# A message-passing layer: where TensorE makes a node block's two products, ahead of the node product of layer one or behind layer two

## The chip, the cores and the metric

The kernel runs on one core of one Trainium2 chip. The metric is the time of one execution on the device, in microseconds (us); lower is better. An engine runs its own instructions in the order in which they were written: TensorE (PE, with weight loads as PEld), VectorE (DVE), ScalarE (ACT), GpSimd (POOL), and SyncE (SP), which only issues DMAs here. They wait for each other through semaphores.

## The reference, cut to what matters

```python
gates = (ssp(edge_state @ We1 + be1) @ We2 + be2) * soft_cutoff      # 200000 edges, 64 wide
nodes = node_state[edges].reshape(num_edges, -1)                     # x[src] beside x[dst]
h = ssp(nodes @ Wn1 + bn1) @ Wn2 + bn2
messages = h * gates
message_sum = jnp.zeros_like(node_state).at[edges[:, 1]].add(messages)
new_state = node_state + (ssp(message_sum @ Ws1 + bs1) @ Ws2 + bs2)  # 12500 nodes, 64 wide
x = _layernorm(x + new_state, axis=-1)
```

`ssp(v)` is `softplus(v) - log 2`. The edges come sorted by `dst`, and low nodes have many more edges than high ones.

## The kernel before, in words

The 200000 edges are cut into 391 groups of 512. A loop makes one step for each group; in step `i` the engines work on several groups at once: the gathers of group `i + 3`, layer one of `i + 1`, layer two of `i`, and the scatter of `i - 2`. Nothing is reordered: `manual_schedule` makes each engine's queue follow the source.

What TensorE does in step `i`, in its order before the change:

- L299 and L342: the biases of layer one for `i + 1` (`layer1_bias`) and of layer two for `i` (`layer2_bias`).
- L371 (`scatter`): the messages of group `i - 2` times one-hot columns. DVE adds the result into the table `sums` (L391, `window`, two adds for a group).
- L286 (`transposes`): the gathered rows of group `i + 1` are turned into the PSUM tile `tx`. ACT copies them to SBUF (L294, `xcopy`).
- L304 (`layer1_edge`): the edge product of layer one.
- L337 (`busy_before_node`): a product that nobody reads, made in 221 of the steps, those for which `four(i + 5)` holds (all four rows of a later group are gathered, none is made from columns), from step 91 on. In the steps before that, L641 (`chunk`) stands here: a piece of a table that is built meanwhile.
- L311 (`layer1_node`): the node product of layer one, which reads what L294 copied; in some steps with L314, for rows that DVE and ACT made from columns of `x` (L262, 16 small copies a step on either engine, chosen by L274).
- L349 and L354 (`layer2`): the products of layer two for group `i`, which read the softplus that DVE wrote a step earlier (L333).

POOL does nothing but issue gathers (L204), three or four a step. ACT does L294, its 16 column copies, then the exponential (L325) and the logarithm (L328) of what L311 made. DVE does the two adds into `sums`, the cut and the message (L363, L367, which read layer two), softplus (L333), the one-hot (L280), its column copies.

The nodes are finished in 25 blocks (a first one of 212 nodes, the rest 512). A block begins when the last edge that points into it has been added into `sums`. Its work is a list of parts; `BLOCK_STEPS` says how many steps later each part is done. Two of the parts have a TensorE product: `hidden` (L410, two products of 128x256 that read `sums`; one for the first block), two steps after the block's last edge, and `layer2` of the block (L438, a bias, and L441, two products of 128x128 that read `l_s`, the ssp that DVE wrote in L433), four steps after `hidden`. In a step that has such a part, the list `early` holds it; `part.tensor(tx_tile())` issues the product into a tile of the `tx` ring, and `part.others()` what DVE does with it (L425 and L426, or L445). 24 of the blocks are done within the loop, so 48 of its steps have one product each; the last block comes behind the loop and uses `gh` tiles.

```python
    def busy_before_node(g):
        nc.tensor.matmul(zs[g][:, 1, :HE], we1..., consts[:, :HE], start=True, stop=True, ...)
```

Of the kernel before, what the change touches and what calls it, by code (L numbers as in the profile page):

```python
# [34 lines left out]
AHEAD = 3  # L35
# [5 lines left out]
BEHIND = 5  # L41
# [14 lines left out]
def node_blocks(N):  # L56

    first = N % NB
    assert N > NB and first % 2 == 0 and first <= HE
    sizes = ([first] if first else []) + [NB] * (N // NB)  # L60
    return [(sum(sizes[:i]), n) for i, n in enumerate(sizes)]


def block_steps(N, NG):

    steps = []
    for at, n in node_blocks(N):
        share = sqrt(min(1.0, (at + n) / N))
        spread = sqrt(share * (1.0 - share) / (NG * GE))
        steps.append(ceil(NG * (share + SPREADS * spread)))  # L70
    return steps
# [33 lines left out]
def gnn_resnorm_kernel(ctx: ExitStack, tc: tile.TileContext, a: dict, out: bass.AP, E: int):  # L105
# [30 lines left out]
    def tx_tile():  # L136
        return psum.tile([P, NB], F32, name="tx")
# [54 lines left out]
    def padding(g, k):  # L192
        return g * GE + k % 2 * HE + k // 2 * P >= E
# [15 lines left out]
    def four(g):  # L209
        return g < NG and not any(padding(g, k) or (g, k) in by_columns for k in range(K))  # L210
# [270 lines left out]
    with tc.manual_schedule():  # L481
# [180 lines left out]
        with tc.tile_pool(name="finish", bufs=1) as finish:  # L662
            blocks = list(zip(node_blocks(N), block_steps(N, NG)))
            last = NG - 1
            parts, begun, complete, rest = {}, None, 0, []

            def at(f, g, *more):
                if 0 <= g < NG:
                    f(g, *more)

            def behind_by(i):
                close = last - CLOSE
                return [g for g in ([i - 2] if i <= close else []) + ([i - 1] if i >= close else []) if g >= 0]

            for g in range(LOADS - 1):
                load(g)
            for g in range(2):
                onehot(g)
            lowest(1, NR)
            everywhere(1, NR)  # L680
            clear(0, CHUNKS)
            highest()
            for i in range(-1, last - 1):
                now = parts.pop(i, [])
                early = [part for part in now if part.tensor]
                at(load, i + LOADS)
                if i >= 0:
                    at(gather, i + AHEAD, range(K), [("transposes", i)] if i < BEHIND else ())
                layer1_bias(i + 1)
                at(layer2_bias, i)  # L690
                for n, g in enumerate(behind_by(i)):
                    scatter(g, zs[i + 1][:, 1, HE + 2 * n * W : HE + 2 * (n + 1) * W])
                transposes(i + 1, ("load", i + 1), ("gather", i + 1), ("onehot", i + 1))
                xcopy(i + 1)
                columns(i, 1, finish)
                layer1_edge(i + 1)
                c = chunk_of(i, NCH)
                if c is None and four(i + AHEAD + BEHIND - 3):
                    busy_before_node(i + 1)
                if c is not None:  # L700
                    beside_sums = zs[i + 1][:, 1, HE + 2 * W : HE + 2 * W + P]
                    chunk(c, beside_sums)
                layer1_node(i + 1)
                exps(i + 1)
                logs(i + 1)
                if c is not None:
                    keep_chunk(c, beside_sums)
                read_columns(i + 1, 1)
                for g in behind_by(i):
                    window(g)  # L710
                if c is not None:
                    clear(c, c + 1)
                at(layer2, i)
                for part in early:
                    part.tensor(tx_tile())
                at(hcut, i)
                at(message, i)
                softplus(i + 1)
                for part in early:
                    part.others()  # L720
                at(onehot, i + 3)
                read_columns(i, 0)
                columns(i, 0, finish)
                choose(finish)
                for part in now:
                    if not part.tensor:
                        part.others()
                for action in beside.get(i, []):
                    action()
                complete = i  # L730
                if blocks and complete >= blocks[0][1] - PREPARE and not begun:
                    begun = node_block(*blocks[0][0], finish)
                    begun.pop(0).others()
                if blocks and complete >= blocks[0][1]:
                    steps = next(steps for steps in BLOCK_STEPS if i + steps[-1] < last - 1)
                    for n, part in zip(steps, begun):
                        parts.setdefault(i + n, []).append(part)
                    rest = begun[len(steps) :]
                    blocks.pop(0)
                    begun = None  # L740
            assert len(blocks) == 1 and begun and not parts


            begun.pop(2).others()
            transposes(last, ("load", last), ("gather", last), ("onehot", last))
            xcopy(last)
            layer1_bias(last)
            layer2_bias(last - 1)
            scatter(last - 2, zs[last][:, 1, HE : HE + 2 * W])
            layer1_edge(last)  # L750
            layer1_node(last)
            for some in (edge, node):
                exps(last, some)
                logs(last, some)
            square, variance, root, scale, store = (part.others for part in rest)
            square()
            window(last - 2)
            for g in range(last - 1, last + 1):
                if g not in window_at:
                    window_bases(g)  # L760
            layer2(last - 1)
            layer2_bias(last)
            softplus(last, edge)
            layer2_edge(last)
            softplus(last, node)
            layer2_node(last)
            hcut(last - 1)
            message(last - 1)
            scatter(last - 1, tx_tile()[:, : 2 * W])
            variance()  # L770
            root()
            hcut(last)
            message(last)
            scatter(last, tx_tile()[:, : 2 * W])
            window(last - 1)
            window(last)
            hidden, clamp = begun.pop(0)
            hidden(gh_tile())
            scale()
            clamp()  # L780
            store()
            for part in begun:
                node_part(part)
# [5 lines left out]
    with tc.If(far > 0), tc.tile_pool(name="outside", bufs=1) as o:  # L789
# [7 lines left out]
        with tc.For_i(0, NG, 1) as g:  # L797
# [51 lines left out]
            for b in range(NBL):  # L849
# [5 lines left out]
                part = sums[:D, b * NB : (b + 1) * NB]  # L855
# [90 lines left out]
```

## Time and profile before

| | us |
|---|---|
| median of three runs | 2354.70 |
| lowest and highest of the three | 2352.55, 2364.48 |
| the profiled execution, whole | 2351.35 |
| its span, first to last instruction | 2349.3 |

| engine | busy us | share |
|---|---|---|
| PE | 1986.8 | 85% |
| PEld | 1549.9 | 66% |
| DVE | 1536.7 | 65% |
| ACT | 1511.8 | 64% |
| POOL | 1391.5 | 59% |

The mean granted TensorE clock was 0.964 of full speed. In the profile a line such as "L410 PE MATMUL tx<-sums,consts" names the source line, the engine, the operation, and what it writes and reads. A group's row gives its count, busy time, mean duration of one record in ns, and the engine's idle time ahead of it with what ended that. A product in f32 leaves two records, so the 47 products of `hidden` are 94 records. In a timeline, the first two columns are the start and the length in us; brackets hold the idle time before.

### The profile page before, as it was taken

The numbers are of one execution on the slowest core, as the hardware profiler recorded it, in microseconds if no ns is written. First come the engines' busy times: TensorE is split into PE (matmuls) and PEld (weight loads), VectorE is DVE, ScalarE is ACT, GpSimd is POOL, SyncE is SP. The second block draws the span as 40 slices with busy tenths as digits, with TensorE's granted clock in tenths as the row PEclk, the third lists the DMA queues.
The fourth block names the chain that finished last, engine by engine and source line by source line (L and its number), as shares of the span: only waits on it lengthen the run. The fifth ranks groups of instructions, "written<-read, shape, count | busy, mean of one in ns | idle before, by whom it ended". The sixth has DMA issues, their size and how long they took to land.

```text
span 2349.3 us, 49245 instructions
## 1 busy us (share of the span) xinstructions
PE 1986.8 (85%) x12011; PEld 1549.9 (66%) x12011; DVE 1536.7 (65%) x9110; ACT 1511.8 (64%) x7412; POOL 1391.5 (59%) x1473
## 2 busy tenths in 40 slices
PE   6788888888888888888888888888888888888877
PEld 4676666666666666666666666666666666666665
DVE  4467666666666666666666667666666676667655
ACT  3466667666666666666667667666666666666653
POOL 6556666566666566666656566665666665556550
PEclk8799999999999999999999999999999999999988
DMA  6332232322222222222222222222222222222220
GB/s 190 95 83 71 64 70 57 79 62 74 60 59 57 54 62 54 59 56 61 55 58 63 52 61 63 59 59 58 59 59 59 59 61 60 55 56 59 60 51 13
DMA packets 162385, 149.51 MB, mean 64 GB/s; under 512 B 40564, under 2 KB 112021, under 8 KB 161962
## 3 DMA queue, kind: packets, MB, share of 16 engines
q1 hardware_dynamic: 114650, 96.55, 15.1%
q0 software_dynamic: 47008, 48.23, 10.9%
q8 instruction: 101, 1.65, 0.3%
q14 instruction: 192, 1.57, 0.2%
q10 hardware_dynamic: 434, 1.50, 0.2%
HBM read 136.50 MB, written 9.62 MB: 62 GB/s over the span
## 4 chain that ended last, share of the span: by engine, by line
PE 76%; issue 12%; DVE 6%; ACT 2%; DVEq 2%; another core or an unknown queue 1%; DMA 1%; POOL 0%; ACTq 0%; POOLq 0%
PE z L311 17%; PE gh L354 13%; PE z L371 10%; PE tx L286 9%; PE gh L349 8%; PE z L304 6%; PE z L337 4%; PE gh L342 3%; PE z L299 3%; DVE column L262 2%; DVEq L245 2%; ACT xT L294 1%; PE tx L410 1%; PE z L314 1%
## 5 line engine op out<-in xcount | busy, mean ns | idle before, releaser
L204 POOL DMA_INDIRECT xg<-in_x,src_i x1469 | 1391.3, 947 | 905.6 <-PE tx L286 378.3
L294 ACT COPY xT<-tx 106x512 f32<-106x512 f32 x391 | 228.6, 585 | 736.1 <-PE tx L286 704.6
L311 PE MATMUL z<-xT,wns 106*128 106x256 f32 x1564 | 464.1, 416 | 270.5 <-issue 238.0
L262 ACT COPY column<-xh 128x4 uint8 x6016 | 608.8, 193 | 0.0
L311 PEld LDWEIGHTS z<-xT,wns 106*128 106x128 f32 x1564 | 273.8, 197 | 420.4 <-issue 336.4
L262 DVE COPY column<-xh 128x4 uint8 x6016 | 486.4, 199 | 11.9 <-issue 6.9
L363 DVE TENSOR_TENSOR h<-gh,cut 128x256 f32<-128x256 f32 x391 | 166.0, 425 | 380.3 <-PE tx L286 260.8
L354 PE MATMUL gh<-consts,s 128*128 128x64 f32 x3128 | 400.2, 272 | 0.0
L354 PEld LDWEIGHTS gh<-consts,s 128*128 128x128 f32 x3128 | 389.6, 196 | 0.1
L328 ACT ACTIVATE u<-u,one 128x768 f32<-128x768 f32 x392 | 365.8, 933 | 13.5 <-ACT u L325 0.8
L333 DVE SCALAR_TENSOR_TENSOR s<-u,z 128x768 f32<-128x768 f32 x392 | 369.3, 942 | 0.4 <-issue 0.3
L391 DVE TENSOR_TENSOR sums<-sums,z 64x42 f32 x778 | 149.4, 192 | 325.5 <-issue 243.1
L325 ACT ACTIVATE u<-z 128x768 f32<-128x768 f32 x392 | 314.7, 803 | 47.2 <-PE z L311 25.5
L371 PEld LDWEIGHTS z<-xg,msg 128*128 128x128 f32 x1556 | 208.9, 195 | 140.9 <-issue 123.4
L371 PE MATMUL z<-xg,msg 128*128 128x84 f32 x1556 | 269.9, 297 | 13.6 <-DVE msg L367 13.5
L349 PEld LDWEIGHTS gh<-consts,s 128*128 128x128 f32 x1564 | 218.8, 196 | 92.7 <-DVE s L333 68.3
L349 PE MATMUL gh<-consts,s 128*128 128x128 f32 x1564 | 269.8, 296 | 11.8 <-issue 7.2
L286 PE MATMUL tx<-consts,xg 128*106 128x128 f32 x1564 | 243.9, 280 | 0.0
L304 PE MATMUL z<-eT,consts 128*128 128x256 f32 x782 | 243.7, 395 | 0.0
L286 PEld LDWEIGHTS tx<-consts,xg 128*106 128x106 f32 x1564 | 187.1, 145 | 1.2 <-issue 1.2
L367 DVE TENSOR_TENSOR msg<-gh,h 128x256 f32<-128x256 f32 x391 | 165.9, 424 | 13.4
L342 PE MATMUL gh<-row,ones 3*128 3x512 bf16 x391 | 149.3, 382 | 0.0
(107 smaller groups left out, 1193.4 us busy)
## 6 DMA issues: line engine op xcount, KB each, us to landing
eT<-in_eT SPq DMA_DIRECT2D x195, 256.0 KB
xg<-in_x,src_i POOLq DMA_INDIRECT x1469
wns<-table SPq DMA_DIRECT2D x782, 21.0 KB
table<-tb SPq DMA_DIRECT2D x14, 448.0 KB
side<-in_sides SPq DMA_DIRECT2D x94, 64.0 KB
y<-in_x SPq DMA_DIRECT2D x24, 128.0 KB
out<-y SPq DMA_DIRECT2D x24, 128.0 KB
xh<-in_xh SPq DMA_DIRECT2D x2, 781.5 KB
```

The costliest lines, as they stand in the source:

```text
L204: behind(note(("gather", g), nc.gpsimd.indirect_dma_start(out=xg[:, k, :D], out_offset=None, in_=x, in_offset=bass.IndirectOffsetOnAxis(ap ...
L262: copy(column_tiles[slot].bitcast(U8)[:, 4 * r : 4 * r + 4], xh[:, bass.ds(column_at[queue][j] - xh_at, 4)])
L286: ins = nc.tensor.transpose(tx[:, k, :], xgs[g][:, k, :DW], ident)
L294: note(("xcopy", g), nc.scalar.copy(xT, xTs[g]))
L304: nc.tensor.matmul(zs[g][:, 0, :HE], we1.rearrange("a h d -> a (h d)"), eTs[g], start=False, stop=True, skip_group_check=True)
L311: nc.tensor.matmul(zn, wns[:, g % REST, h, :], xTs[g][:, h], start=True, stop=not chosen, skip_group_check=True)
L325: nc.scalar.activation(us[g][:, part], z_of(g)[:, part], AF.Exp)
L328: nc.scalar.activation(us[g][:, part], us[g][:, part], AF.Ln, bias=one)
L333: nc.vector.scalar_tensor_tensor(ss[g].rearrange("p i t e -> p (i t e)")[:, part], us[g][:, part], BIG, z_of(g)[:, part], OP.min, OP.max)
L349: nc.tensor.matmul(v[:, 0, t], ss[g][:, 0, t, :], we2, start=False, stop=False, skip_group_check=True)
L354: nc.tensor.matmul(ghs[g][:, 1, 2 * t + h, :], ss[g][:, 1 + h, t, :], wn2, start=False, stop=h == 1 and t == 1, skip_group_check=True)
L371: ins = nc.tensor.matmul(sc, msgs[g][:, 2 * t : 2 * t + 2, :].rearrange("p h f -> p (h f)"), xgs[g][:, 2 * t : 2 * t + 2, D:DW], start=t = ...
```

## The change

In the 48 steps with a block's product, the product is issued between the edge product L304 and the node product L311 of layer one, where it stood behind layer two (L354). The unread product L337 is not made in such a step, where it was made before.

```diff
                 layer1_edge(i + 1)
                 c = chunk_of(i, NCH)
-                if c is None and four(i + AHEAD + BEHIND - 3):
+                for part in early:
+                    part.tensor(tx_tile())
+                if c is None and not early and four(i + AHEAD + BEHIND - 3):
                     busy_before_node(i + 1)
                 if c is not None:
                     beside_sums = zs[i + 1][:, 1, HE + 2 * W : HE + 2 * W + P]
...
                 at(layer2, i)
-                for part in early:
-                    part.tensor(tx_tile())
                 at(hcut, i)
                 at(message, i)
                 softplus(i + 1)
```

The unread product is made 221 times before and 190 times after: 31 of the 48 steps had it. The other 17 gain a product in that place.

TensorE's queue around a step with `hidden` (L410), before; the names are those of the tiles: `z` layer one, `gh` layer two, `tx` the transposes and the blocks, `xT` what ACT copied:

```order
L371 MATMUL z<-xg,msg 128x84 x2
L286 MATMUL tx<-consts,xg 106x128 x4
L304 MATMUL z<-eT,consts 128x256
L337 MATMUL z<-consts 128x256
L311 MATMUL z<-xT,wns 128x256 x2
L349 MATMUL gh<-consts,s 128x128 x2
L354 MATMUL gh<-consts,s 128x64 x4
L410 MATMUL tx<-sums,consts 128x256 x2
L299 LDWEIGHTS be_82
```

The same step with the change:

```order
L371 MATMUL z<-xg,msg 128x84 x2
L286 MATMUL tx<-consts,xg 106x128 x4
L304 MATMUL z<-eT,consts 128x256
L410 MATMUL tx<-sums,consts 128x256 x2
L311 MATMUL z<-xT,wns 128x256 x2
L349 MATMUL gh<-consts,s 128x128 x2
L354 MATMUL gh<-consts,s 128x64 x4
L299 LDWEIGHTS be_82
```

L410 takes the place of L337, and L299 of the next step follows layer two at once. Since the adds into `sums` of step `i` (L391) are written behind this place, L410 now reads `sums` as the adds of step `i - 1` left it; by then the block's last edges are in.

DVE's queue in such a step, with the semaphores that each row waits for, before:

```order
L391 TENSOR_TENSOR sums<-sums,z 64x42 [waits Activation_49]
L391 ISA
L391 TENSOR_TENSOR sums<-sums,z 64x42
L363 TENSOR_TENSOR h<-gh,cut 128x256 [waits PE_49]
L367 TENSOR_TENSOR msg<-gh,h 128x256 [waits DVE_49]
L333 SCALAR_TENSOR_TENSOR s<-u,z 128x768 [waits Activation_49]
L425 TENSOR_SCALAR l_s<-tx,consts 128x256 [waits PE_49]
L426 TENSOR_SCALAR zb<-tx,consts 128x256
```

And with the change:

```order
L391 TENSOR_TENSOR sums<-sums,z 64x42 [waits Activation_49]
L391 ISA
L391 TENSOR_TENSOR sums<-sums,z 64x42
L363 TENSOR_TENSOR h<-gh,cut 128x256 [waits PE_49]
L367 TENSOR_TENSOR msg<-gh,h 128x256 [waits DVE_49]
L333 SCALAR_TENSOR_TENSOR s<-u,z 128x768 [waits Activation_49]
L425 TENSOR_SCALAR l_s<-tx,consts 128x256
L426 TENSOR_SCALAR zb<-tx,consts 128x256
```

Only the wait of L425 for TensorE is gone. The adds L391, which may write `sums` only once L410 has read it, wait as before for the exponential of the same step, which follows L311 and so L410. The order on ACT, POOL and SP is the same in both.

## The prediction

> **What bounds the kernel now.** I read the page's chain of waits first, then the timeline of ACT, POOL and PE in a quiet stretch, then the groups and the waits of the two block products.
>
> ```profile
> PE 76%; issue 12%; DVE 6%; ACT 2%; DVEq 2%; another core or an unknown queue 1%; DMA 1%; POOL 0%; ACTq 0%; POOLq 0%
> PE z L311 17%; PE gh L354 13%; PE z L371 10%; PE tx L286 9%; PE gh L349 8%; PE z L304 6%; PE z L337 4%; PE gh L342 3%; PE z L299 3%; DVE column L262 2%; DVEq L245 2%; ACT xT L294 1%; PE tx L410 1%; PE z L314 1%
> ```
>
> By this TensorE sets the time: its products fill three quarters of the chain. But L337, which nobody reads, has 4% of it, so the chain also runs through products that only fill a wait. The rhythm says more. The copy xT (L294) runs once a step; these are its starts in five steps without a block product, and the gathers between them (the first and the last of each run, or its last alone):
>
> ```profile
> 1599.21 0.58 ACT L294 COPY xT<-tx 106x512 f32<-106x512 f32 x1 [1.57 <-PE tx L286]
> 1603.93 0.59 ACT L294 COPY xT<-tx 106x512 f32<-106x512 f32 x1 [0.95 <-PE tx L286]
> 1609.88 0.58 ACT L294 COPY xT<-tx 106x512 f32<-106x512 f32 x1 [2.18 <-PE tx L286]
> 1614.75 0.59 ACT L294 COPY xT<-tx 106x512 f32<-106x512 f32 x1 [1.11 <-PE tx L286]
> 1620.56 0.59 ACT L294 COPY xT<-tx 106x512 f32<-106x512 f32 x1 [2.03 <-PE tx L286]
> ...
> 1601.88 0.94 POOL L204 DMA_INDIRECT xg<-in_x,src_i  x1 [0.30 <-issue]
> 1604.05 0.94 POOL L204 DMA_INDIRECT xg<-in_x,src_i  x1 [1.22 <-PE tx L286]
> ...
> 1607.79 0.94 POOL L204 DMA_INDIRECT xg<-in_x,src_i  x1 [0.30 <-issue]
> 1610.05 0.94 POOL L204 DMA_INDIRECT xg<-in_x,src_i  x1 [1.32 <-DVE sums L391]
> ...
> 1612.55 0.94 POOL L204 DMA_INDIRECT xg<-in_x,src_i  x1 [0.30 <-issue]
> 1614.72 0.94 POOL L204 DMA_INDIRECT xg<-in_x,src_i  x1 [1.23 <-PE tx L286]
> ...
> 1618.46 0.94 POOL L204 DMA_INDIRECT xg<-in_x,src_i  x1 [0.30 <-issue]
> ```
>
> A step with a run of three gathers takes 4.72 us (1599.21 to 1603.93) or 4.87, one with four 5.95 or 5.81. The difference is about one gather (0.94 + 0.30). Each time the copy starts 1.1 to 1.2 us behind the end of the run's last gather (1602.82 to 1603.93, 1608.73 to 1609.88, 1613.49 to 1614.75, 1619.40 to 1620.56), and the next run starts beside it. So POOL and TensorE go round together. Over the record of all copies,
>
> ```profile
> L294 ACT COPY xT<-tx x391: 563/585/587, 26.0 to 2326.9; 106x512 f32<-106x512 f32 x196
> ```
>
> sorted by the gathers that start between two of them, from 576 us on and without block products: 64 intervals with three gathers, median 4.72, and 124 with four, mean 6.03. What TensorE itself needs for a round is seen in the three-gather steps, where its copy does not wait: about 4.6 to 4.7. In a four-gather step it has 1.3 us to spare. It spends them here:
>
> ```profile
> 1603.73 0.60 PE L304 MATMUL z<-eT,consts 128*128 128x256 f32 x2
> 1604.57 1.13 PE L311 MATMUL z<-xT,wns 106*128 106x256 f32 x4 [0.24 <-issue]
> ...
> 1619.16 0.60 PE L304 MATMUL z<-eT,consts 128*128 128x256 f32 x2
> 1619.59 0.59 PE L337 MATMUL z<-consts 128*128 128x256 f32 x2
> 1621.20 1.13 PE L311 MATMUL z<-xT,wns 106*128 106x256 f32 x4 [1.01 <-issue]
> ```
>
> In the three-gather step L311 follows the edge product after 0.24 us, when the copy is done. In the four-gather step L304 ends at 1619.76, and 1.44 us go by: L337, then 1.01 of nothing.
>
> **What is moved, and its price now.** The moved instructions are matmuls and their weight loads alone: no DMA, no work of DVE, ACT, POOL or SP.
>
> ```profile
> L410 PE MATMUL tx<-sums,consts 128*128 128x256 f32 x94 | 28.2, 425 | 26.6 <-DVE sums L391 21.9 <-issue 4.4
> L441 PE MATMUL tx<-consts,l_s 128*128 128x128 f32 (+1 forms) x96 | 17.7, 307 | 0.0
> L438 PE MATMUL tx<-rs,ones 3*128 3x256 bf16 (+1 forms) x24 | 6.7, 279 | 0.0
> L337 PE MATMUL z<-consts 128*128 128x256 f32 x442 | 136.8, 392 | 0.0
> ```
>
> `hidden` costs 28.2 / 24 = 1.2 us a block, the second product 24.4 / 24 = 1.0, and TensorE stands 26.6 us ahead of L410, waiting for the adds into `sums` of its own step. On TensorE's row that is 79 us. How much of it lengthens the kernel is read from the intervals.
>
> *The second product (L438, L441).* Two steps with it, one of four gathers (first pair), one of three:
>
> ```profile
> 1343.99 0.59 ACT L294 COPY xT<-tx 106x512 f32<-106x512 f32 x1 [2.24 <-PE tx L286]
> 1350.08 0.58 ACT L294 COPY xT<-tx 106x512 f32<-106x512 f32 x1 [2.32 <-PE tx L286]
> ...
> 1647.83 0.58 ACT L294 COPY xT<-tx 106x512 f32<-106x512 f32 x1 [2.27 <-PE tx L286]
> 1653.41 0.58 ACT L294 COPY xT<-tx 106x512 f32<-106x512 f32 x1 [1.81 <-PE tx L286]
> ```
>
> 6.09 against 6.03: with four gathers it is hidden, 16 times. 5.58 against 4.72 with three, six times; the interval behind comes out 0.4 shorter, so 0.45 is lost each time: 2.7 us in all.
>
> *`hidden` (L410).* The clearest case:
>
> ```profile
> 1622.74 1.00 PE L354 MATMUL gh<-consts,s 128*128 128x64 f32 x8
> 1625.52 1.36 PE L410 MATMUL tx<-sums,consts 128*128 128x256 f32 x4 [1.77 <-DVE sums L391]
> ...
> 1623.49 1.19 DVE L274 SCALAR_TENSOR_TENSOR chosen<-side,column 64x128 f32<-64x128 int32 x4
> 1624.97 0.40 DVE L391 TENSOR_TENSOR sums<-sums,z 64x42 f32 x2 [0.28 <-issue]
> ...
> 1629.59 0.58 ACT L294 COPY xT<-tx 106x512 f32<-106x512 f32 x1 [5.26 <-PE tx L286]
> ...
> 1602.40:1626.20 23.80, 19.35 (x120) 14.75 (x120) 16.74 (x101) 15.54 (x77) 14.64 (x16) 1.00 0.27 63
> 1626.20:1633.10 6.90, 6.90 (x22) 5.06 (x22) 3.71 (x22) 2.10 (x17) 3.21 (x4) 0.51 0.22 59
> 1633.10:1660.00 26.90, 23.79 (x153) 18.87 (x152) 17.68 (x98) 18.92 (x87) 15.63 (x17) 1.00 0.24 53
> ```
>
> Layer two is done at 1623.74; DVE, late with `chosen`, adds into `sums` only until 1625.37; TensorE stands 1.77 us, and behind that its clock is half (0.51 in the stretch from 1626.2 to 1633.1) for almost 7 us. The interval is 1620.56 to 1629.59, 9.03 against 6.03. I took for each of the 21 `hidden` between 576 and 2222 us the interval that holds it and the three behind it, less 6.03 or 4.72 each: from nothing (seven are under 0.2) to 4.4, together 32.0 us. Ten are followed by a half-clock stretch of this kind and have 26.5 of it. The one before 576 us adds 0.6.
>
> The Trainium skill ("TensorE: Matmul & The Clock Gate", "What's actually happening") says that the clock halves after a whole idle window of about 3.4 us. Here it halved after a wait of 1.77, so the measurement decides. If by that rule the half clock came from elsewhere and stayed, the sum below would lose the part of the 26.5 that is not waiting: the ten wait some 19.5 us, so an estimate of 7.
>
> **The price in the new place.** With four gathers the gap between L304 and L311 is 1.44 us; `hidden` is two products of L337's shape, which starts 0.43 behind L304, so it takes 0.86. The second product takes 0.21 + 0.67 = 0.88 of the chain, as here:
>
> ```profile
> 2230.64 0.21 PE tx L438
> 2230.85 0.67 PE tx L441 x4
> ```
>
> L337 goes, and nothing moves: cost nothing; without that cover it would be 0.9 each. With three gathers, 17 times, L311 starts late by 0.62 (eight `hidden`) or 0.64 (nine of the others), 10.7 us in all if every one counted, nothing if the next interval has four gathers and its 1.3 us to spare. All of them but the last three have that, so I take nothing for these. The wait is new in one respect: L410 now stands ahead of L311 and the step's exponential, logarithm and softplus, and waits for the adds of the step before. These ran before the edge product's end in 18 of the 24 steps; the worst is 1.0 us late, and with the gap that leaves 0.35. Nothing again; 1 us at most over all.
>
> In the last 100 us the gathers are over or nearly so, and a scatter takes the step's own message:
>
> ```profile
> 2292.44 1.15 PE L371 MATMUL z<-xg,msg 128*128 128x84 f32 x4 [3.00 <-DVE msg L367]
> 2316.61 0.68 PE L371 MATMUL z<-xg,msg 128*128 128x84 f32 x4 [0.55 <-DVE msg L367]
> ```
>
> There the products behind layer two ran while TensorE would wait for that message. In front they delay it: three times by 0.6, some 2 us, 4 if the clock is half. I take 2.
>
> **Sum**, against the profiled execution's 2351.35: 32.0 + 0.6 + 2.7 - 2 = 33.3 us less, 2318. The profiled execution lies 3.4 under the median and 1.2 under the lowest of the runs, so a median would be 2321 and a lowest run 2319; I say **2320**.
>
> **Rivals.**
>
> *A. All of TensorE's row comes off*, as the chain's 76% would have it: 26.6 + 52.6 = 79, so 2276. Against it: the second product hides within 0.06 us in four-gather steps, and L337 would have to matter too. 0.07.
>
> *B. The waits move on and nothing is left.* DVE is what is late at L410, and the next products that it feeds are L371 and L349. If TensorE meets the same lateness there, 32 us stay; 2.7 less 2 is no change: 2354. For it: in the case above DVE's softplus ended at 1627.4, late against its usual place. Against: DVE stood idle ahead of L363 in most steps, so it catches up within a step if TensorE does not wait, and four-gather steps have 1.3 us to spare. 0.13.
>
> *C. Slower.* As B, at one place: L349, which waits for softplus; and there the lateness adds to the late L311 of the 17 steps without L337, since both lie ahead of layer two. Then 10.7 and the end's 4 come on top and the 2.7 doesn't show: 2354.7 + 14.7 = 2369. It decides once more than about 20 of the 26.6 us are found again ahead of L349 and L311 starts late in steps whose next run has three gathers. Against: among the 17, only three have such a run behind them, all of them after 2260 us. 0.10.
>
> **How the numbers follow.** My forecast has 0.70, A 0.07, B 0.13, C 0.10. A measurement of this kernel can tell about 0.5%, 12 us, from no change. The forecast's own range is 2308 (11 us more in the end phase and in stretches of half clock that I didn't count) to 2333 (10.7 and 2 more lost). To leave out no more than 2 in 10, A, C and a little, it takes in B and some more below: 2302 to 2356. Faster: forecast and A, 0.77; same: B, 0.13; slower: C, 0.10.
>
> **What would show it.** Right: L410 with little idle ahead of it; L438 and L441 as busy as before; L337 380 records; intervals with a block product at 6.0 and 4.7; far fewer half-clock stretches between 780 and 2210 us, so a mean clock above 0.964; L311's idle time smaller by about what the 48 gaps took. Wrong: half-clock stretches at the same steps with the wait ahead of L349 or L371 (B, C); copies xT that start late where a product in front has no run of four gathers behind it (C); three-gather steps under 4.6 (A).

## The result, and the profile after

The changed kernel took 2328.2 us (median of 6 runs, 2325.8 to 2330.0), the kernel before 2355.9 beside it (6 runs, 2352.6 to 2364.5): a ratio of 0.988, with a 95% interval from 0.9865 to 0.9895. In a later group of runs it came to 2328.5 against 2358.6, ratio 0.987 (0.985 to 0.989). The forecast was 2320. The gain is 28 to 30 us instead of 33, and well clear of no change.

The profiled execution of the change took 2329.9 us (span 2328.0, mean granted clock 0.972, where before had 0.964). Its chain of waits, by engine and by line:

```profile
PE 75%; issue 13%; DVE 5%; ACT 2%; DVEq 2%; another core or an unknown queue 1%; POOL 1%; DMA 1%; ACTq 0%; POOLq 0%
PE z L311 17%; PE gh L354 13%; PE z L371 9%; PE gh L349 8%; PE tx L286 8%; PE z L304 6%; PE gh L342 3%; PE z L337 3%; PE z L299 3%; DVEq L245 1%; DVE column L262 1%; PE tx L410 1%; PE z L314 1%; DVE h L363 1%
```

The chain hardly tells the two kernels apart. The groups do (count, then busy time and mean ns of one, then the idle time of the engine just ahead of them and what ended it):

```profile
L311 PE MATMUL z<-xT,wns 106*128 106x256 f32 x1564 | 463.5, 415 | 297.8 <-issue 262.1 <-ACT xT L294 32.0 <-ACT rstd L457 1.2
L371 PE MATMUL z<-xg,msg 128*128 128x84 f32 x1556 | 266.4, 294 | 17.6 <-DVE msg L367 17.5
L349 PE MATMUL gh<-consts,s 128*128 128x128 f32 x1564 | 271.5, 297 | 9.0 <-issue 3.5 <-DVE s L333 3.0 <-DVE msg L367 1.4
L337 PE MATMUL z<-consts 128*128 128x256 f32 x380 | 114.4, 383 | 0.0
L410 PE MATMUL tx<-sums,consts 128*128 128x256 f32 x94 | 26.3, 404 | 3.8 <-DVE sums L391 3.3 <-PE tx L286 0.4
L441 PE MATMUL tx<-consts,l_s 128*128 128x128 f32 (+1 forms) x96 | 18.1, 313 | 2.5 <-DVE l_s L433 1.4 <-issue 1.1
```

Before, three of these rows were:

```profile
L311 PE MATMUL z<-xT,wns 106*128 106x256 f32 x1564 | 464.1, 416 | 270.5 <-issue 238.0 <-ACT xT L294 30.3 <-ACT l_s L430 0.5
L371 PE MATMUL z<-xg,msg 128*128 128x84 f32 x1556 | 269.9, 297 | 13.6 <-DVE msg L367 13.5
L349 PE MATMUL gh<-consts,s 128*128 128x128 f32 x1564 | 269.8, 296 | 11.8 <-issue 7.2 <-DVE s L333 3.5
```

TensorE's idle time ahead of `hidden` (L410) went from 26.6 to 3.8 us. It did not come back ahead of L371 and L349, which together have 26.6 where they had 25.4. L311 waits longer, 297.8 us where it was 270.5, but not in the steps that hold a block product. Of the steps between 576 and 2222 us that `four(i + 5)` picks out, those with `hidden` in front have 0.41 us ahead of L311 (1.03 before); the next two have 0.95 and 1.37 (0.00 and 0.44 before). With the second product it is 0.51 (1.13 before), and 0.95 (0.19) in the step behind. So the wait grew in the steps that follow a block product: TensorE no longer comes to them late, and waits for the copy there as in any other step (median 1.08 in both kernels).

At about the place of the prediction's clearest case the timeline of the change reads (start, length; in brackets the engine's idle time ahead and what ended it):

```profile
1619.63 1.03 PE L410 MATMUL tx<-sums,consts 128*128 128x256 f32 x4
1620.76 0.58 ACT L294 COPY xT<-tx 106x512 f32<-106x512 f32 x1 [2.15 <-PE tx L286]
1621.40 1.13 PE L311 MATMUL z<-xT,wns 106*128 106x256 f32 x4 [0.74 <-issue]
1622.94 1.00 PE L354 MATMUL gh<-consts,s 128*128 128x64 f32 x8
1626.79 0.58 ACT L294 COPY xT<-tx 106x512 f32<-106x512 f32 x1 [2.26 <-PE tx L286]
```

and the three stretches that the prediction showed of before (length, then busy time and count of PE, PEld, DVE, ACT and POOL, then the granted clock, the DMA share and GB/s):

```profile
1602.40:1626.20 23.80, 21.35 (x133) 16.17 (x132) 16.04 (x98) 15.59 (x77) 14.61 (x16) 1.00 0.26 64
1626.20:1633.10 6.90, 5.16 (x33) 3.95 (x32) 4.61 (x27) 4.91 (x22) 3.81 (x5) 1.00 0.29 68
1633.10:1660.00 26.90, 23.40 (x148) 18.03 (x149) 18.75 (x114) 18.94 (x96) 16.94 (x18) 1.00 0.26 60
```

`hidden` now runs inside the gap ahead of L311 and leaves 0.74 us of it. The interval between the copies is 6.03 us, as in a step without a block product; it was 9.03. The clock is 1.00 where it was 0.51.

**Where the time went, by the prediction's own count.** For every execution that follows I added up, as the prediction did, what each interval between copies xT has over 6.03 us (four gathers) or 4.72 (three). The block whose `hidden` falls at about 1325 us is kept apart, since its place is disturbed in every execution for a reason of its own, shown in the last section.

| us | `hidden`, without that block | second product | that block | other | to the 93rd copy | half-clock stretches, 540 to 2222 us |
|---|---|---|---|---|---|---|
| before | 29.7 | 2.9 | 2.3 | 2.7 | 576.4 | 13 |
| the change | 2.0 | 0.8 | 5.4 | 1.9 | 581.9 | 3 |
| the change again | 2.5 | 0.9 | 7.6 | 2.5 | 582.8 | 2 |
| only `hidden` in front | 2.5 | 2.9 | 7.3 | 4.6 | 578.7 | 3 |
| only the second product in front | 26.0 | 1.0 | 3.4 | 2.0 | 577.9 | 10 |
| the change, unread product kept | 3.1 | 1.0 | 5.3 | -0.2 | 575.2 | 4 |
| before, 31 unread products left out | 35.7 | 13.3 | 2.2 | 3.5 | 577.8 | 18 |
| before, `hidden` without adds | 3.9 | 3.6 | 3.1 | 0.8 | 580.9 | 3 |
| before, filler ahead of `hidden` | 19.7 | 3.7 | 7.9 | 2.3 | 575.5 | 4 |
| the change, end as before | 2.3 | 1.3 | 5.7 | 0.8 | 581.5 | 3 |

From before to the change: 27.7 us off `hidden`, 2.1 off the second product, 0.8 off other places, 3.1 on at the one block, 5.5 on ahead of the 93rd copy and 1.0 on at the end, 21 in all, which is the difference of the two spans (2349.3 and 2328.0).

### The profile page after: what moved, and what is told of

It reads as the page before. It is cut to its first block, busy times and chain, and to the rows that moved or that the text cites. A ratio compares the mean times of both kernels' runs of the same rounds, so it can differ in the third digit from the quotient of the medians.

```text
span 2328.0 us, 49147 instructions
## 1 busy us (share of the span) xinstructions
PE 1954.9 (84%) x11949; PEld 1526.4 (66%) x11949; DVE 1535.9 (66%) x9110; ACT 1513.0 (65%) x7412; POOL 1390.1 (60%) x1473
## 3 DMA queue, kind: packets, MB, share of 16 engines
q14 instruction: 192, 1.57, 0.2%
## 4 chain that ended last, share of the span: by engine, by line
PE 75%; issue 13%; DVE 5%; ACT 2%; DVEq 2%; another core or an unknown queue 1%; POOL 1%; DMA 1%; ACTq 0%; POOLq 0%
PE z L311 17%; PE gh L354 13%; PE z L371 9%; PE gh L349 8%; PE tx L286 8%; PE z L304 6%; PE gh L342 3%; PE z L337 3%; PE z L299 3%; DVEq L245 1%; DVE column L262 1%; PE tx L410 1%; PE z L314 1%; DVE h L363 1%
## 5 line engine op out<-in xcount | busy, mean ns | idle before, releaser
L311 PE MATMUL z<-xT,wns 106*128 106x256 f32 x1564 | 463.5, 415 | 297.8 <-issue 262.1
L311 PEld LDWEIGHTS z<-xT,wns 106*128 106x128 f32 x1564 | 273.1, 196 | 441.7 <-issue 368.1
L354 PE MATMUL gh<-consts,s 128*128 128x64 f32 x3128 | 400.7, 272 | 0.0
L354 PEld LDWEIGHTS gh<-consts,s 128*128 128x128 f32 x3128 | 390.3, 196 | 0.1
L391 DVE TENSOR_TENSOR sums<-sums,z 64x42 f32 x778 | 150.6, 194 | 328.2 <-issue 253.0
L371 PEld LDWEIGHTS z<-xg,msg 128*128 128x128 f32 x1556 | 206.0, 192 | 143.6 <-issue 121.6
L371 PE MATMUL z<-xg,msg 128*128 128x84 f32 x1556 | 266.4, 294 | 17.6 <-DVE msg L367 17.5
L349 PEld LDWEIGHTS gh<-consts,s 128*128 128x128 f32 x1564 | 218.2, 196 | 93.0 <-DVE s L333 69.7
L349 PE MATMUL gh<-consts,s 128*128 128x128 f32 x1564 | 271.5, 297 | 9.0 <-issue 3.5
L304 PE MATMUL z<-eT,consts 128*128 128x256 f32 x782 | 238.7, 388 | 0.0
```

The costliest lines, as they stand in the source:

```text
L304: nc.tensor.matmul(zs[g][:, 0, :HE], we1.rearrange("a h d -> a (h d)"), eTs[g], start=False, stop=True, skip_group_check=True)
L311: nc.tensor.matmul(zn, wns[:, g % REST, h, :], xTs[g][:, h], start=True, stop=not chosen, skip_group_check=True)
L349: nc.tensor.matmul(v[:, 0, t], ss[g][:, 0, t, :], we2, start=False, stop=False, skip_group_check=True)
L354: nc.tensor.matmul(ghs[g][:, 1, 2 * t + h, :], ss[g][:, 1 + h, t, :], wn2, start=False, stop=h == 1 and t == 1, skip_group_check=True)
L371: ins = nc.tensor.matmul(sc, msgs[g][:, 2 * t : 2 * t + 2, :].rearrange("p h f -> p (h f)"), xgs[g][:, 2 * t : 2 * t + 2, D:DW], start=t = ...
```

## The experiments

Theory 1 was the prediction's: a run of gathers on POOL paces the steps, and what `hidden` cost was its wait and the half clock behind it. Theory 2 was that TensorE's row is the bound and each product counts.

**Only `hidden` in front.** Edit, against the kernel before:

```diff
+                ahead = [part for part in early if part.tensor.__name__ == "hidden"]
+                for part in ahead:
+                    part.tensor(tx_tile())
-                if c is None and four(i + AHEAD + BEHIND - 3):
+                if c is None and not ahead and four(i + AHEAD + BEHIND - 3):
...
                 for part in early:
-                    part.tensor(tx_tile())
+                    if part not in ahead:
+                        part.tensor(tx_tile())
```

> Only the product `hidden` (L410) goes in front, and takes the place of the unread product in its own step; the second product (L438, L441) stays behind layer two, and its step keeps the unread product where it had one. Theory 1 (the round of POOL and TensorE paces the steps; what `hidden` cost was its wait of 26.6 us for the adds of its own step and the half clock behind that): nearly all of the gain of the change is here, 23 to 27 us under the kernel before (ratio 0.9885 to 0.990); L410 idle under 5 us, second product in three-gather steps still 5.5 to 5.6 us an interval. Theory 2 (TensorE's row is the bound, and each product that isn't done counts): 26.6 of waiting and about 16 L337 less at 0.6 each, some 36 us (ratio 0.985).

Measured: 2330.5 us against 2351.6, ratio 0.9895 (0.987 to 0.992), 21 us less. The group of `hidden`:

```profile
L410 PE MATMUL tx<-sums,consts 128*128 128x256 f32 x94 | 25.5, 394 | 3.8 <-DVE sums L391 3.2 <-PE tx L286 0.4 <-issue 0.3
```

The second product keeps its 2.9 in the table. The ratio is the one that theory 1 gave, though 21 us is a little under its 23 to 27; theory 2's 0.985 lies outside the interval.

**Only the second product in front.** The same edit with "layer2" for "hidden".

> Only the second product (L438, L441) goes in front, in place of the unread one; `hidden` stays behind layer two. Theory 1: only the 2.7 us of the second product in three-gather steps come off, 2 to 4 us under before (0.998 to 0.999); L410 idle 26 us and the half-clock stretches behind it as before. Theory 2: some 15 L337 at 0.6 and their weight loads come off, 10 us or more (0.996 or less). If this kernel gained as much as the change (0.988), the place of the second product would be the cause, and my account of `hidden` false.

Measured: 2352.9 us against 2351.6, ratio 0.9997 (0.998 to 1.0015). The group of `hidden`:

```profile
L410 PE MATMUL tx<-sums,consts 128*128 128x256 f32 x94 | 28.8, 432 | 27.9 <-DVE sums L391 22.6 <-issue 5.0
```

In the table the 2.9 us go to 1.0 and `hidden` keeps 26.0. In the three-gather steps the interval falls from 5.57 to 4.70, so theory 1's 2 us are there step by step; in the time they are lost in the scatter. Theory 2's 0.996 or less lies outside the interval. The two halves together show that the gain is `hidden`'s.

**The change with the unread product kept** in the 31 steps, behind the block product:

```diff
-                if c is None and not early and four(i + AHEAD + BEHIND - 3):
+                if c is None and four(i + AHEAD + BEHIND - 3):
```

> The change with the unread product L337 kept behind the block product in its 31 steps. Theory 1: with four gathers 1.44 us are free ahead of L311; 0.9 of block product and 0.6 of L337 make about 1.5, so almost nothing is lost: within 4 us of the change (0.987 to 0.990 of before). Theory 2 (each product on TensorE counts): 31 L337 of 0.6 us, 13 to 19 us above the change (0.994 to 0.996 of before).

Measured: 2334.5 us, ratio 0.992 (0.9896 to 0.9944). The profiled execution was the quickest of its six, 2321.9 us, and by the table nothing is added in its steps. The ratio lies between the two theories; the change itself was not in this group (in its own two it had 0.988 and 0.987). Whether these products cost nothing or some 10 us stays open. They don't bring anything.

**The kernel before with the 31 unread products left out**, the block products staying behind layer two:

```diff
-                if c is None and four(i + AHEAD + BEHIND - 3):
+                if c is None and not early and four(i + AHEAD + BEHIND - 3):
```

> The kernel before with its products behind layer two, and L337 left out in the 31 steps. Theory 1: nothing comes off, since L337 fills a wait there: within 2 us of before (0.999 to 1.001); L410 idle about 26 us as before, and L311 idle larger by about 31 x 0.6. Theory 2: 13 to 19 us under before (0.992 to 0.9945).

Measured: 2366.6 us against 2351.6, ratio 1.0055 (1.003 to 1.008): less work, and 15 us slower. Neither theory had this. One of these steps, of three gathers and with the second product, in this kernel (timeline of TensorE, then three stretches):

```profile
1428.69 0.60 PE L304 MATMUL z<-eT,consts 128*128 128x256 f32 x2
1430.86 2.03 PE L311 MATMUL z<-xT,wns 106*128 106x256 f32 x4 [1.57 <-issue]
...
1425.00:1431.00 6.00, 4.43 (x29) 3.38 (x30) 4.50 (x26) 3.79 (x22) 3.84 (x5) 0.99 0.30 73
1431.00:1434.30 3.30, 3.30 (x13) 2.93 (x13) 2.64 (x20) 2.66 (x16) 2.24 (x3) 0.50 0.43 99
1434.30:1442.00 7.70, 7.46 (x50) 5.92 (x51) 4.03 (x24) 4.58 (x21) 3.83 (x4) 1.00 0.27 63
```

and the same step in the kernel before:

```profile
1423.30 0.60 PE L304 MATMUL z<-eT,consts 128*128 128x256 f32 x2
1423.73 0.59 PE L337 MATMUL z<-consts 128*128 128x256 f32 x2
1425.46 1.13 PE L311 MATMUL z<-xT,wns 106*128 106x256 f32 x4 [1.14 <-issue]
```

Without L337 TensorE stands 1.57 us instead of 1.14, and then L311 takes 2.03 us instead of 1.13 at a clock of 0.50. So the unread product is worth more than its time: it keeps TensorE busy enough for the full clock. In the change the block product stands in the gap and does the same (3 half-clock stretches, where this kernel has 18), with work that is wanted. Left out with nothing in its place, it costs. In the table both columns rise (2.9 to 13.3, 29.7 to 35.7).

**`hidden` in its old place, without the adds to wait for.** The blocks within the loop read a constant tile instead of `sums`:

```diff
+                moving = sums[:, first + q * HE : first + (q + 1) * HE] if first + n == N else consts[:, :HE]
                 nc.tensor.matmul(t["z"], ws1[:, q].rearrange("f o d -> f (o d)"),
-                                 sums[:, first + q * HE : first + (q + 1) * HE], start=q == 0, stop=q == nq - 1,
+                                 moving, start=q == 0, stop=q == nq - 1,
```

> The kernel before in everything, but `hidden` of the blocks within the loop reads a constant tile instead of `sums` (so the node outputs of these blocks are other numbers), so that it has no adds to wait for. Theory 1 (its wait for the adds of its own step, and the half clock behind that wait, are what the change took away, not the place): L410's idle falls from 26.6 to under 6 us, at most four half-clock stretches are left between 540 and 2222 us (13 before, 3 with the change), and the time is 18 to 26 us under before (0.989 to 0.992). What is left of the change's gain is then the late L299 and transposes behind `hidden` in three-gather steps, 2 us or so. Rival (the place behind layer two itself costs, whatever `hidden` waits for): under 10 us of gain (0.996 or more).

Measured: 2332.1 us against 2358.6, ratio 0.9897 (0.988 to 0.992), 26.5 us less. Its group of the product in question (L411 there):

```profile
L411 PE MATMUL tx<-consts 128*128 128x256 f32 x94 | 25.5, 393 | 0.0
```

No idle time, three half-clock stretches, and 3.9 us left of `hidden`. The ratio lies in theory 1's range, and the rival's 0.996 lies outside the interval. The place behind layer two costs next to nothing; the wait that it brings was the cost.

**Two unread products directly ahead of `hidden`**, in its old place, on the tile that it then overwrites:

```diff
+            for _ in range(2 if first + n != N else 0):
+                nc.tensor.matmul(t["z"], we1.rearrange("a h d -> a (h d)"), consts[:, :HE], start=True, stop=True,
+                                 skip_group_check=True)
```

> The kernel before, with two more unread products of L337's kind (0.43 to 0.6 us each) directly ahead of `hidden`, on the tile that it then overwrites, in the blocks within the loop: TensorE is busy through half or more of the wait for the adds, while the wait itself ends no earlier. The kernel without 31 of its unread products came out 0.55% slower, with half-clock stretches behind a gap of 1.57 us ahead of L311, so an unread product can be worth its time by keeping the clock. Theory 1a (most of what `hidden` cost is the half clock; the wait alone mostly fits the 1.3 us of slack of a four-gather step): half-clock stretches fall from 13 to 6 or fewer, 12 to 22 us under before (0.9905 to 0.995). Theory 1b (the wait itself lengthens the round): 0 to 7 us under before (0.997 to 1.000). Rival (TensorE's row counts): 48 more products, 10 us or more above before.

Measured: 2348.0 us against 2358.6, ratio 0.996 (0.994 to 0.998): 48 more products and 10 us less. The clearest case of the prediction in this kernel (filler L410, `hidden` L413):

```profile
1625.07 1.00 PE L354 MATMUL gh<-consts,s 128*128 128x64 f32 x8
1625.91 1.08 PE L410 MATMUL tx<-consts 128*128 128x256 f32 x4
1627.35 0.40 DVE L391 TENSOR_TENSOR sums<-sums,z 64x42 f32 x2 [0.34 <-issue]
1627.81 1.13 PE L413 MATMUL tx<-sums,consts 128*128 128x256 f32 x4 [0.82 <-issue]
1630.44 0.59 ACT L294 COPY xT<-tx 106x512 f32<-106x512 f32 x1 [3.78 <-PE tx L286]
```

The adds still end when they end, and `hidden` (1.13 us, at full clock) still waits for them. The interval, from the copy at 1622.89, is 7.55 us: it was 9.03 with the half clock and is 6.03 with the change. So half of this case's 3 us was the clock, and half the wait. Over all blocks the table says 29.7, 19.7 and 2.0: at least 10 us were the clock and at most 18 the wait. At one block (2042 us here) the half clock is still there, with 4.5 of the 19.7, and where the wait was shorter than the two fillers they lengthen the step themselves (from 0.92 to 1.32 us too much at one block). The ratio falls just between theories 1a and 1b, which is what such a split means.

**The change with the last three block products left behind layer two**:

```diff
-                for part in early:
+                ahead = [part for part in early if i <= last - CLOSE]
+                for part in ahead:
...
+                for part in early:
+                    if part not in ahead:
+                        part.tensor(tx_tile())
```

> The change, but in the last steps, where a scatter takes the step's own message, three block products stay behind layer two and the unread product keeps its place. My forecast took 2 us (4 at half clock) for these three in front. Theory 1: 1 to 4 us under the change (0.998 to 0.9995 of it); steps 374 to 387 in the profile about 90 us against 91.8. Rival (the end is paced by something else, as its 90.8 us of before and 91.8 of the change say): no difference that can be measured, within 1 us.

Measured: 2327.9 us, the change beside it 2328.5; ratios to before 0.988 (0.986 to 0.990) and 0.987 (0.985 to 0.989). Between the 375th and the 388th copy it took 90.2 us; the change had 91.8 and 91.6, before 90.8. The 2 us that the forecast took for the end phase are about what the profile has (1.4 to 1.6), and too small to be seen in the time: 0.6 us, as the rival has it. The change itself, in the same group:

> The changed kernel itself once more, beside the others of this group on one chip. The kernel with the unread product kept (0.992) and the one with `hidden` alone in front (0.9895) came out close to the change's 0.988; if these differ only by scatter, the change repeats at 0.987 to 0.991, and the profiled execution's first 92 steps (581.9 us in the first profile; 575 to 579 in the four other kernels, which do not differ there but for two blocks) come back to 575 to 580. If the 0.992 of the kernel with L337 kept is a cost of those products, this one stays at 0.988 or under.

Its 0.987 is in the range. The expectation about the first 93 copies failed: 582.8 us again. But the kernel with the unread product kept has the same instructions up to there, and took 575.2; so one program scatters there by 7 us. Of the lateness against before, 4.0 us in the first profile and 6.0 in this one are there by the 55th copy, ahead of the first block product, so the new place isn't what makes them.

**Three gathers a step.** The change, and the kernel before, with the fourth gather of each group replaced by a fill with zeros:

```diff
-            if padding(g, k) or (g, k) in by_columns:
+            if padding(g, k) or (g, k) in by_columns or k == K - 1 and four(g):
```

> The change with the fourth gather of every group that has four replaced by a DVE fill with zeros (so the groups' fourth part is computed on other data, and the outputs are other numbers); TensorE's work is the same. Theory 1 (the run of gathers on POOL paces the step: 4.72 us with three, 6.03 with four): the 210 four-gather steps between step 92 and 374 fall to 4.7 to 4.9 us, 240 to 340 us under the change together with the steps ahead of 92 (0.85 to 0.90 of before). Rival (TensorE's row, 84% busy with 1955 us, is the bound, and its idle time stays what it is): less than 60 us (over 0.96 of before).

> The kernel before with the same fill in place of the fourth gathers (outputs other numbers in the same way). The 1.3 us of slack that TensorE has in a four-gather step are then gone. Theory 1: like the change's counterpart 240 to 330 us under before, but the products behind layer two are nowhere hidden: 35 to 60 us above the change's counterpart (the change itself gained 28 to 30). Rival (the cost of the two products behind layer two doesn't hang on the slack): 25 to 31 us above it.

and the change with all gathers and without any unread product from the 93rd step on (the condition gets "and i < 92"):

> The change with every unread product L337 from step 92 on left out. My prediction held that L337 only fills a wait, and that its going costs nothing; leaving it out in 31 steps of the kernel before cost 0.55% (half-clock stretches behind gaps of 1.57 us ahead of L311). Theory 1 with that finding (an unread product or a block product in the gap keeps the clock; a gap of 1.5 us or more may halve it): 20 to 100 us above the change, many half-clock stretches between 540 and 2222 us. Rival (it only fills a wait in steps without a block product): within 5 us of the change.

In this group the kernel before, unaltered, took 1946.7 us (15 runs, 1943.0 to 1950.0). Beside it the change with three gathers took 1910.6, ratio 0.982; before with three gathers 1943.2, ratio 0.9985; the change without unread products 1911.0, ratio 0.982. In the groups before this one, a copy xT whose transposes ended within a run of gathers mostly started only behind that run (the last section counts it): the signal of TensorE came late. Here it doesn't. The last of these kernels has all its gathers; its copies, gathers, transposes and node products:

```profile
1304.63 0.95 POOL L204 DMA_INDIRECT xg<-in_x,src_i  x1 [0.30 <-DMA xg<-in_x,src_i]
1305.28 0.60 PE L286 MATMUL tx<-consts,xg 128*106 128x128 f32 x4
1305.88 0.94 POOL L204 DMA_INDIRECT xg<-in_x,src_i  x1 [0.30 <-issue]
1305.91 0.59 ACT L294 COPY xT<-tx 106x512 f32<-106x512 f32 x1 [0.28 <-PE tx L286]
1306.55 1.13 PE L311 MATMUL z<-xT,wns 106*128 106x256 f32 x4 [0.24 <-ACT xT L294]
1307.13 0.95 POOL L204 DMA_INDIRECT xg<-in_x,src_i  x1 [0.30 <-issue]
1308.38 0.94 POOL L204 DMA_INDIRECT xg<-in_x,src_i  x1 [0.30 <-DMA xg<-in_x,src_i]
...
1310.47 0.59 ACT L294 COPY xT<-tx 106x512 f32<-106x512 f32 x1 [0.79 <-PE tx L286]
```

The transposes end at 1305.88, and the copy starts at 1305.91, while a gather runs. In the profile of before it started 1.2 us behind the transposes (median of 282 steps), here 0.04. The steps take 4.56 us whether three gathers run in them or four. In this group the copies didn't wait for the end of a run of gathers, and the whole kernel was 17% faster; the program of before is the same one. So the group says nothing of theory 1 where the signals are late. The change with three gathers ran in one more group:

> The change with three gathers a step once more (the fourth filled with zeros by DVE, so outputs of other numbers). In the group before, the kernel before itself took 1946.7 us instead of 2351 to 2358: TensorE's signals came through at once there (the copy xT 0.04 us behind the last transpose, and not 0.9 to 1.3), and four-gather steps took 4.56 us with all four gathers, so that this kernel told nothing of the pace there. If the kernel before takes about 2355 us in this group: theory 1 (the signals come through only behind a run of gathers, so its length paces the step) 240 to 340 us under the change's 2328, that is 0.85 to 0.90 of before, with the copy xT still 0.9 us or more behind the transposes wherever TensorE is the earlier; rival (the signals are late for another reason, whatever the number of gathers): steps stay at 5.8 us or more, over 0.96 of before. If before takes about 1946 us again: 0.982 of it, as in the group before, and nothing told apart.

Before took 1946.4 us again, and this kernel 1908.4, ratio 0.981. Whether fewer gathers would shorten the steps where the signals are late wasn't tried: none of these two groups met that condition.

What the group does show is the price of the block products where TensorE is the bound (PE busy 97% of the span with three gathers in the change). A step takes 4.56 us without one, 4.92 with `hidden` in front and 6.00 behind layer two, 4.93 with the second product in front and 5.44 behind. Change against before, both with three gathers, comes to 32.6 us, nearer to the rival (25 to 31) than to my 35 to 60; it is what these prices make of the 21 and 20 blocks past the 93rd copy, 21 x 1.08 + 20 x 0.51 = 33. And the unread product, which keeps the clock in the first condition, is without effect in this one: 1910.6 with it and 1911.0 without. These two kernels differ in the fourth gather too, which made 3.5 us between the two kernels of before (1946.7 and 1943.2). So this fits the rival's "within 5 us", but only in this condition; the change with both, unread products and four gathers, was not timed in it.

## Why the prediction was right, and where it was off

*The mechanism.* Right. `hidden` alone brings 21 us (ratio 0.9895 to the change's 0.988), and taking away what it waits for brings 26.5 without moving it. It is not that products were taken off TensorE's row: the 31 unread ones, left out alone, make the kernel 15 us slower. What no run here shows is that the gathers pace the steps. The intervals of 4.72 and 6.03 us go with three and four gathers, but the kernels with fewer gathers were timed only where the copy doesn't wait for them.

*The term of 32.0 + 0.6 for `hidden`.* This is the step that was mis-sized: 24.7 us net. In it was the block at 1325 us with 2.3, whose lateness comes from POOL; it is not taken away, and it grew to 5.4 (7.6 in the second execution). Another block, at 1975 us of the change, keeps 1.3 of its 2.9: its `hidden` doesn't wait in front, but POOL pauses there too, 2.81 us (last section). I had counted whatever an interval near a `hidden` had too much as that product's. The other 19 gave back what was counted, but for 0.7 us in all. So the mechanism held, and the size was off, since not all that was late at a `hidden` was late because of it. The 0.6 ahead of 576 us can't be seen under the scatter there.

*Half clock.* Right that it came from these waits: 13 stretches fell to 3 with the change and to 3 where `hidden` had no adds to wait for. The prediction weighed a rule of the Trainium skill ("TensorE: Matmul & The Clock Gate", "What's actually happening"), by which an idle window of about 3.4 us is needed, and 7 us, by its estimate, would have stayed behind. They didn't stay; the measurement decides. The run with fillers puts the clock's part of the cost at 10 us or more.

*The second product.* 2.7 forecast, 2.1 in the intervals. I had counted six steps of three gathers; by the gathers of their groups it is four between 576 and 2222 us (5.56 to 5.59 us each) and one behind. Hidden in four-gather steps: right, with the interval behind it none of the 16 has over 0.15 us too much, before or after.

*The new place costs nothing.* Right: between 576 and 2222 us the three-gather steps with a block product in front take 4.69 to 4.72 us and the next one 5.96 to 6.08, but for the two blocks named above. But the reason that I gave was half of one. "L337 goes, and nothing moves" holds since the block product is in the gap in its place; L337 gone and nothing in its place costs 15 us. I had read the unread product as one that only fills a wait. It also holds the clock.

*The idle time ahead of L311.* It was to fall by what the gaps took, as a sign of being right. It fell in the steps with a block product, as said, but grew by 27.3 us in all. I had overlooked that TensorE came late to the steps behind those, and had no idle time there.

*The end phase.* 2 us forecast; in the profiles 1.0 against before, and 1.4 to 1.6 against the change with its end as before.

*The rest.* The profiled execution of the change came to the 93rd copy 5.5 us late; 4.0 of these stand ahead of the first block product, so they are scatter, and for the other 1.5 nothing tells scatter from cost. Its 2329.9 us and the forecast's 2318 for a profiled execution differ by 12: 5.5 of the start, 7.9 of `hidden`'s term, 0.6 of the second product, less 1.0 at the end and 0.8 elsewhere.

*The rivals.* A (the whole row, 2276) fell where the signals are late; where they are not, TensorE is the bound, and there too the difference (with three gathers in both kernels) was 33 us and not 79. B and C fell: the idle time ahead of L349 and L371 together grew by 1.2 us only.

## What to carry to other kernels

Before an instruction is moved on a busy engine, ask what it waits for in its place, and count the interval that holds it, not its own duration: here 1.2 us of product cost up to 5 us of step. Then ask what the thing that it replaces did besides its own work; an unread product can be what keeps the clock, and it may go only where something else fills the same gap. And let a change that rests on one pacing be timed in more than one group of runs, for the pacing itself may not be there in the next.

## What the runs showed that I had not expected

*Signals behind a run of gathers.* In the change, at the block that stayed late:

```profile
1326.12 0.94 POOL L204 DMA_INDIRECT xg<-in_x,src_i  x1 [2.71 <-issue]
...
1328.53 0.60 PE L286 MATMUL tx<-consts,xg 128*106 128x128 f32 x4
...
1333.61 0.94 POOL L204 DMA_INDIRECT xg<-in_x,src_i  x1 [0.30 <-issue]
1334.66 0.59 ACT L294 COPY xT<-tx 106x512 f32<-106x512 f32 x1 [5.23 <-remote]
1335.30 2.08 PE L311 MATMUL z<-xT,wns 106*128 106x256 f32 x4 [5.31 <-issue]
```

POOL pauses 2.71 us (3.73 in the kernel before, and 2.81 at another block of the change, below; what for, no row says) and then issues two steps' gathers, seven in a row. The transposes end at 1329.13, the last gather at 1334.55, and the copy of what was transposed starts 0.11 behind that. By these times a longer run holds the signal longer: 5.5 us here, 1.2 in a usual step. In before the second run at that place waited for something else for 1.26 us, and the copy came through in the pause. So a kernel with less waiting can lose time at such a place, 3 us here. The other block:

```profile
1975.50 0.58 ACT L294 COPY xT<-tx 106x512 f32<-106x512 f32 x1 [2.19 <-PE tx L286]
...
1977.15 0.99 POOL L204 DMA_INDIRECT xg<-in_x,src_i  x1 [2.81 <-issue]
...
1981.46 0.58 ACT L294 COPY xT<-tx 106x512 f32<-106x512 f32 x1 [2.19 <-PE tx L286]
```

A step of three gathers, and 5.96 us long: its run starts late by the pause.

The same shows over the 282 copies that the table covers, in the profiled execution of the change. For 189 of them the transposes end while a run of gathers goes on. All but four of these copies start only behind the run (median 1.34 us behind the transposes); the four have transposes that end within 0.6 us of the run's start. The other 93 have a median of 0.04 us. That it is TensorE's signal which is held up, and by what, is inferred from these times; no run changes the runs of gathers alone where it happens.

*The same program without them.* In the last two groups of runs the copy followed the transposes by 0.04 us, though in the kernel with all gathers 213 of 282 transposes end while a gather runs, and the kernel before took 1946 us; in all the others it took 2352 to 2359, with 1.2 us at the copy. The results number the chips 7 and 6 for the first two groups of experiments, and 6 and 10 for the last two, so the number doesn't tell them apart. What makes the difference stays open.

*What halves the clock.* The record of the granted clock comes in stretches that are multiples of 3.41 us. Over ten profiled executions (of the two kernels first compared and of the first two groups of experiments), from 540 to 2222 us, I cut each into windows of that length and compared the share of a full-clock window in which a matmul ran with the clock of the next window. Halved: 23 of 23 under 0.5, 14 of 19 from 0.5 to 0.55, 11 of 34 from 0.55 to 0.6, 5 of 103 from 0.6 to 0.65, and 10 of 4644 above. So a window need not be idle; a wait of about 1.5 us on top of the usual gaps can be enough (1.57 and 1.77 us in the steps shown), and by these counts it hangs on how much of one window is idle, and so on how the wait lies in it. The same wait of 1.5 to 1.7 us was followed by a halved clock 15 times in 39, which that would explain.
